# A two-layer attention and expert kernel: the next layer norm's statistics beside the attention's tail, loads reordered, bias products on two row groups, a division shared by two engines

## The chip, the cores and the metric

The kernel runs on one core of a Trainium2 chip. The metric is the device time of one execution in microseconds (us). Beside the times there is one execution recorded by the hardware profiler, from which all durations here come. PE is TensorE's matrix unit and PEld its weight loads, DVE is VectorE, ACT ScalarE, POOL GpSimd, SP SyncE; SP issues most of the transfers.

## The reference

The input x has 2 sequences of 2048 tokens with 256 channels. Two layers follow one another, each of the form

```
xn = layernorm(x)
x  = x + attention(xn) * silu(ffn(xn))
```

```python
# layer 0: full attention over 2048 tokens, 16 heads of 16 channels, scale 1/sqrt(256)
# its ffn: 2 branches of 8 experts of rank 64
xV = einsum('btd,kdr->btkr', Q_side, V);  yW = einsum('btd,kdr->btkr', K_side, W)
prod = xV * cumsum(yW, axis=1)
weights = softmax(gelu(Q_side @ router_w1.T + b1) @ router_w2.T + b2 + expert_bias)
out = einsum('btkr,kdr->btd', prod * weights[..., None], U) + weights @ b
ffn = ((out_fwd + alpha * out_inv) / n_valid) @ W_O.T
# layer 1: attention over the keys at most 64 positions away, scale 1/sqrt(16)
# its ffn: a base product and 8 low-rank experts of rank 16
gate = softmax(xt @ gate_w.T)
ffn  = xt @ weight.T + (1/16) * einsum('ne,eor,ner->no', gate, lora_V, einsum('nh,erh->ner', xt, lora_U))
```

All of it is in 32-bit floats.

## The kernel before

Channels lie on the 128 partitions (two halves, `c`), tokens on the free axis, in blocks of 512 (`TB`): four blocks for each of the two sequences (`b`). Three arrays stay in the on-chip memory: `x`, `xn` (the normed input, later the attention's result) and `gt` (the gate silu(ffn)). A 32-bit product is two passes on TensorE, so the profile counts twice as many matmuls as the code. Tiles come from rotating pools, and an instruction waits until the slot that its tile takes has been read. Each engine works its instructions in a fixed order, and so does each queue of transfers; a scheduler settles this order when the program is built, from the order of the calls, except where `keep_in_program_order` (`pin`) holds an instruction in place.

**Start.** ScalarE's queue loads `wq`, `wiT`, `wk`, `r1T`; SP's queue loads the blocks of x (`load_x`, L54) with the other weights between them. The first products (L204) fold the weights into one another: `wiT` with `wq`, then with `wk`. Beside them `layer_norms` goes over the eight blocks: transposes of x into PSUM (L104), statistics on VectorE (L108 to L115), scaling on ScalarE (L121), transposes back (L127) and copies into `xn` (L129). One of these products multiplies the experts' biases with W_O and gives `bO`, 16 rows. SP then loads the attention's weights and biases and fills rows of the array `qd` in device memory.

**Layer 0's experts.** After the router, a loop over the eight blocks multiplies eight chunks (`px` L387, `py` L391, `po` L371), with the routing weights broadcast from device memory (`we`). Each block ends with two products of `bO` (16 rows) with `wT` (L403), one for each half of the channels, both added into `po`.

**Attention.** `attention` is called once per layer. Its work is cut into 32 items `(b, g, n)`: sequence, group of four heads, block of queries. The four heads sit on partitions 0, 32, 64 and 96. An item has `U` steps, 16 in layer 0, 2 in layer 1. Two streams run side by side: for an item ahead, scores `sq` with queries on the partitions, of which VectorE takes the maxima (L617 in layer 0, the masked `seen` at L612 in layer 1); for the present item, scores `sk` with keys on the partitions (L605), exponentials on ScalarE (L621), in layer 1 masks on POOL (L626), and the products with the values, `acc` (L664). `place_max` transposes an item's maxima (`pmx`, L642), VectorE writes them negated into `row` (L644), and a transfer puts them into the queries as an extra row. In layer 0 the `acc` of the steps are added up in `av`: ScalarE copies each out of PSUM (`more`, L674) and POOL adds it (L675). A table `after`, filled by `at(step, f, ...)`, says behind which step the later parts are called: `away`, `compact`, `invert`, `write`, `spread` and `divide` send an item's sums through device memory and divide (`divide`, L717, on POOL in layer 0, on VectorE in layer 1); `project` multiplies with `wo` (L750), VectorE multiplies with `gt` (L755), POOL adds to x (L756), and in layer 1 the block goes out. The last items (one in layer 0, three in layer 1) are divided by `last_there` and `last_back` instead, with transposes on TensorE (L725, L742).

```python
hops = (0, 1, 3, 4, 5, 7, 8) if local else (0, 2, 4, 5, 7, 11, 13)
...
for s in range(-(U + LEAD), max(after) + 1):
    ...
    scores(divmod(s, U) if 0 <= s < total else None, divmod(s1, U) if s1 < total else None, es)
    ...
    for f, args in after.get(s, []):
        f(*args)
```

With `LEAD` 3, the stream of maxima is `U + 3` steps ahead, so layer 0's last 19 steps have scores `sk`, exponentials and `acc` alone.

**Between the layers.** When the first attention is over, layer 1's weights are loaded, `layer_norms` goes over all eight blocks again, with the gate's logits beside it (`gates` L849, `tokens` L860, `normalized`, `turned` L876), and `turned` sends the gates through device memory to be broadcast (`ge`). Then `experts` takes the blocks: `pt` (L887), the base product (L893), `tg` on VectorE (L889), the second low-rank product (L897), silu on ScalarE (L899). The second attention starts with its keys and queries (`pp`, L456) and values (L469).

Of the kernel before, what the change touches and what calls it, by code (L numbers as in the profile page):

```python
# [17 lines left out]
P = 128  # L18
# [19 lines left out]
def two_layers(ctx: ExitStack, tc: tile.TileContext, a, out):  # L38
# [20 lines left out]
    load_x(0, 0)  # L59
# [13 lines left out]
    def load_attn(pool, l, eng):  # L73
        return dict(
            q=load(pool, f"wq{l}", [P, NC, D], rows(a[f"wq{l}"]), eng),
            k=load(pool, f"wk{l}", [P, NC, D], rows(a[f"wk{l}"]), eng),
            v=load(pool, f"wv{l}", [P, NC, D], rows(a[f"wv{l}"]), eng),
            o=load(pool, f"wo{l}", [P, NC, D], rows(a[f"wo{l}"]), eng),
            bq=load(pool, f"bq{l}", [P, NC], a[f"bq{l}"], eng),
            bk=load(pool, f"bk{l}", [P, NC], a[f"bk{l}"], eng),  # L80
            bo=load(pool, f"bo{l}", [P, NC], a[f"bo{l}"], eng),
            bv=load(pool, f"bv{l}", [P, NC], a[f"bv{l}"], eng),
        )
# [10 lines left out]

    def layer_norms(blocks, tmp, ps, between=lambda r: None):


        QT = TB // P

        def there(b, n):  # L100
            xt = ps.tile([P, QT, D], F32, name="xt", tag="xt")
            for t in range(QT):
                for c in range(NC):
                    nc.tensor.transpose(xt[:, t, bass.ts(c, P)], x[b][:, c, bass.ds(n * TB + t * P, P)], ident)  # L104
            st = tmp.tile([P, QT, 6], F32, name="st", tag="st")
            mv = tmp.tile([P, QT, 2], F32, name="mv", tag="mv")
            for t in range(QT):
                nc.vector.bn_stats(st[:, t, :], xt[:, t, :])  # L108
            for t in range(QT):
                nc.vector.bn_aggr(mv[:, t, :], st[:, t, :])  # L110

            f = tmp.tile([P, 2, QT], F32, name="f", tag="f")
            nc.scalar.activation(f[:, 0, :], mv[:, :, 1], AF.Sqrt, bias=eps_t)
            nc.vector.reciprocal(f[:, 0, :], f[:, 0, :])
            nc.vector.scalar_tensor_tensor(f[:, 1, :], mv[:, :, 0], -1.0, f[:, 0, :], ALU.mult, ALU.mult)  # L115
            return b, n, xt, f
# [15 lines left out]
        for r in range(len(blocks) + 1):  # L132
            first = there(*blocks[r]) if r < len(blocks) else None
            if held:
                back(*held)
            held = first
            between(r)
# [12 lines left out]
    layer0 = ctx.enter_context(ExitStack())  # L150
    wat0 = layer0.enter_context(tc.tile_pool(name="wat0", bufs=1))

# [6 lines left out]
    with tc.tile_pool(name="fw", bufs=1) as fw:  # L159
# [4 lines left out]
        bO = fw.tile([2 * KE, D], F32, name="bO")  # L164
# [4 lines left out]
        with tc.tile_pool(name="raw", bufs=1) as raw, tc.tile_pool(name="tn", bufs=2) as tn, tc.tile_pool(  # L169
# [3 lines left out]
            wq = load(raw, "wq", [P, NC, D], rows(a["W_Q"]), nc.scalar)  # L173
            wiT = load(raw, "wiT", [P, NC, D], rows(a["W_invT"]), nc.scalar)
            wk = load(raw, "wk", [P, NC, D], rows(a["W_K"]), nc.scalar)
# [14 lines left out]
            bT = load(raw, "bT", [P, NC, 2 * KE], rows(a["bT"]), nc.sync)  # L190
# [32 lines left out]
            product(lambda m: bO, bT, 2 * KE, woT)  # L223
# [10 lines left out]
        A0 = load_attn(wat0, 0, nc.sync)  # L234
# [13 lines left out]
        nc.vector.reciprocal(rn, rn)  # L248
        ones = fw.tile([P, TB], F32, name="ones")
# [13 lines left out]
        with tc.tile_pool(name="pa", bufs=2, space=PSUM) as pa, tc.tile_pool(  # L263
# [87 lines left out]
            with tc.tile_pool(name="ta", bufs=2) as ta:  # L351
                for b in range(B):
                    prev = None
                    for n in range(NB):
# [9 lines left out]
                        wT = ta.tile([2 * KE, TB], F32, name="wT", tag="wT")  # L364
                        nc.sync.dma_start(out=wT, in_=wd[b][:, cols])
# [36 lines left out]
                        for oc in range(NC):  # L402
                            nc.tensor.matmul(po[oc], bO[:, bass.ts(oc, P)], wT, start=False, stop=True)  # L403
# [12 lines left out]
    def attention(A, scale, local, final):  # L416
# [14 lines left out]
        with ExitStack() as st:  # L431
# [204 lines left out]
            def place_max(i):  # L636
# [6 lines left out]
                row = mp.tile([NG * TT, P], F32, name="row", tag="row")  # L643
                nc.vector.tensor_scalar(row, ps, -1.0, None, ALU.mult)  # L644
# [5 lines left out]
            def weigh(i, u, es):  # L650
# [17 lines left out]
                if local:  # L668
                    nc.scalar.copy(avs[i][:, bass.ts(u, 2 * P)], acc[:, : 2 * P])
                elif u == 0:  # L670
# [42 lines left out]
            def divide(i):  # L713

                b, g, n = items[i]
                pin(
                    (nc.vector if local else nc.gpsimd).tensor_tensor(together(b, g, n), together(b, g, n), divs.pop(i), ALU.mult)  # L717
                )
# [26 lines left out]
            def project(i, oc):  # L745
# [10 lines left out]
                nc.gpsimd.tensor_tensor(x[b][:, oc, cols], x[b][:, oc, cols], up, ALU.add)  # L756
                if final and oc == NC - 1:
# [12 lines left out]
            for i, (b, g, n) in enumerate(items):  # L770
# [5 lines left out]
                if i >= len(items) - (3 if local else 1):  # L776

                    hops, steps = (0, 1, 2), (last_there, last_back)
                for hop, f in zip(hops, steps):
                    at(end + DEL + hop, f, i)  # L780
# [5 lines left out]
                if n == NB - 1:  # L786
                    at(end, fetch, b * NG + g + 2, T // 2 if local else 0)
            fetch(0)
# [34 lines left out]

    attention(A0, 1.0 / float(np.sqrt(D)), False, False)
    layer0.close()


    wat1 = ctx.enter_context(tc.tile_pool(name="wat1", bufs=1))
    A1 = load_attn(wat1, 1, nc.sync)
    with tc.tile_pool(name="gw", bufs=1) as gw, tc.tile_pool(name="tb", bufs=2) as tb, tc.tile_pool(  # L830
        name="gdp", bufs=1, space=bass.MemoryType.DRAM
    ) as gdp:
        gateT = gw.tile([P, NC, HP], F32, name="gateT")
        nc.vector.memset(gateT, 0.0)
        nc.scalar.dma_start(out=gateT[:, :, :KE], in_=rows(a["gateT"]))
        baseT = load(gw, "baseT", [P, NC, D], rows(a["weightT"]), nc.scalar)
        lU = load(gw, "lU", [P, NC, KE * R1], rows(a["lUT"]), nc.scalar)
        lV = load(gw, "lV", [KE * R1, D], a["lVT"], nc.scalar)
        lg = gw.tile([P, B * NT, KE], F32, name="lg1")
# [3 lines left out]

        def gates(pool, b, n):

            pl = pool.tile([P, P], F32, name="pl1", tag="s")
            for c in range(NC):
                for t in range(TB // P):
                    nc.tensor.matmul(  # L849
                        pl[t * HP : (t + 1) * HP, :], gateT[:, c, :], xn[b][:, c, bass.ds(n * TB + t * P, P)],  # L850
                        start=(c == 0), stop=(c == NC - 1),
                    )
            sl = tb.tile([P, P], F32, name="sl", tag="sl")
            nc.vector.tensor_copy(sl, pl)
            return b, n, sl

        def tokens(pool, b, n, sl):

            pt = pool.tile([P, P], F32, name="plt", tag="s")
            nc.tensor.transpose(pt, sl, ident)  # L860
            t0 = (b * NB + n) * (TB // P)
            nc.vector.tensor_copy(
                lg[:, t0 : t0 + TB // P, :], pt.rearrange("p (t w) -> p t w", w=HP)[:, :, :KE]
            )

        def normalized(b):
            lgb = lg[:, b * NT : (b + 1) * NT, :]
            rec = softmax8(gw, lgb, NT, "g")
            nc.vector.tensor_scalar(rec, rec, 1.0 / R1, None, ALU.mult)
            nc.vector.tensor_tensor(lgb, lgb, rec[:, :, None].to_broadcast([P, NT, KE]), ALU.mult)  # L870

        def turned(pool, b):
            for n in range(NB):
                pw = pool.tile([KE, TB], F32, name="pw1", tag="s")
                for t in range(TB // P):
                    nc.tensor.transpose(pw[:, bass.ts(t, P)], lg[:, (b * NB + n) * (TB // P) + t, :], ident)  # L876
# [6 lines left out]
        def experts(pool, b, n):  # L883
            cols = bass.ts(n, TB)
            pt = pool.tile([P, TB], F32, name="pt", tag="a")
            for c in range(NC):
                nc.tensor.matmul(pt, lU[:, c, :], xn[b][:, c, cols], start=(c == 0), stop=(c == NC - 1))  # L887
            tg = tb.tile([P, TB], F32, name="tg", tag="tg")
            nc.vector.tensor_tensor(tg, ge[b][:, cols], pt, ALU.mult)  # L889
            po = [pool.tile([P, TB], F32, name=f"po1{oc}", tag="o", bufs=4) for oc in range(NC)]  # L890
# [5 lines left out]
            for oc in range(NC):  # L896
                nc.tensor.matmul(po[oc], lV[:, bass.ts(oc, P)], tg, start=False, stop=True)  # L897
                gs = gt[b][:, oc, cols]
                nc.scalar.activation(gs, po[oc], AF.Silu)  # L899

                nc.vector.scalar_tensor_tensor(
                    x[b][:, oc, cols], gs, A1["bo"][:, oc : oc + 1], x[b][:, oc, cols], ALU.mult, ALU.add
                )

        with tc.tile_pool(name="pn1", bufs=2, space=PSUM) as pn1, tc.tile_pool(
            name="pg1", bufs=2, space=PSUM
        ) as pg1:
            blocks = [(b, n) for b in range(B) for n in range(NB)]
            held = {}

            def between(r):
                if r - 1 in held:
                    tokens(pg1, *held.pop(r - 1))
                if 1 <= r <= len(blocks):
                    held[r] = gates(pg1, *blocks[r - 1])
                if r == NB + 1:
                    normalized(0)
                if r == NB + 3:
                    turned(pg1, 0)

            layer_norms(blocks, tb, pn1, between)
# [82 lines left out]
```

## Time and profile before

| | |
|---|---|
| time, median of 3 runs | 2598.02 us (2597.92 to 2598.47) |
| profiled execution: its own time | 2595.75 us |
| its span, first to last instruction | 2594.0 us |
| granted TensorE clock, mean | 0.997 |
| busy: PE, DVE, ACT, POOL | 2543.6, 1681.6, 1633.7, 893.3 us |
| start to the first matmul | 8.21 us |
| layer 0's experts, from 131 on | to 478 us |
| first attention's steps | about 590 to 2121 us |
| layer norm, gates and experts of layer 1 | 2121 to 2236 us |
| second attention's steps | about 2330 to 2573 us |

A row of a view by stages gives a stretch, its length, and the busy time of PE, PEld, DVE, ACT and POOL with the number of instructions, then the granted clock, the share of the DMA engines and GB/s. A row of the timeline gives the start, the duration, the engine, the line, the operation, and in brackets how long the engine had been idle and what ended this. A row of the waits gives who waited for whom, the sum in us, the number of times and the longest.

### The profile page before, as it was taken

The numbers are of one execution on the slowest core, as the hardware profiler recorded it, in microseconds if no ns is written. First come the engines' busy times: TensorE is split into PE (matmuls) and PEld (weight loads), VectorE is DVE, ScalarE is ACT, GpSimd is POOL, SyncE is SP. The second block draws the span as 40 slices with busy tenths as digits, with TensorE's granted clock in tenths as the row PEclk, the third lists the DMA queues.
The fourth block names the chain that finished last, engine by engine and source line by source line (L and its number), as shares of the span: only waits on it lengthen the run. The fifth ranks groups of instructions, "written<-read, shape, count | busy, mean of one in ns | idle before, by whom it ended". The sixth has DMA issues, their size and how long they took to land.

```text
span 2594.0 us, 48140 instructions
## 1 busy us (share of the span) xinstructions
PE 2543.6 (98%) x18916; PEld 1075.1 (41%) x18916; DVE 1681.6 (65%) x2755; ACT 1633.7 (63%) x3188; POOL 893.3 (34%) x836
## 2 busy tenths in 40 slices
PE   8999999999999999999999999999999988999998
PEld 5444444543333333333333333333333325467765
DVE  4143333258888888888777888888888714138875
ACT  5400000127888888888878888888888874236654
POOL 0000000102444444444444444444444440107776
PEclk9999999999999999999999999999999999999999
DMA  7031111320001001010000001010000012234542
GB/s 246 37 85 49 50 49 33 121 74 3 16 10 49 12 11 47 12 44 16 10 22 36 12 21 37 12 46 14 10 16 12 10 34 35 73 123 129 157 143 85
DMA packets 80098, 129.83 MB, mean 50 GB/s; under 512 B 27456, under 2 KB 32448, under 8 KB 77056
## 3 DMA queue, kind: packets, MB, share of 16 engines
q1 hardware_dynamic: 77824, 125.19, 15.4%
q8 instruction: 148, 2.42, 0.4%
q10 hardware_dynamic: 2048, 1.58, 0.2%
q14 instruction: 78, 0.64, 0.1%
HBM read 80.23 MB, written 45.97 MB: 49 GB/s over the span
## 4 chain that ended last, share of the span: by engine, by line
PE 93%; DVE 3%; DMA 2%; ACT 1%; issue 1%; POOL 0%; POOLq 0%; ACTq 0%; SPq 0%; DVEq 0%
PE sk L605 24%; PE acc L664 21%; PE sq L605 18%; PE pp L456 4%; PE py L391 4%; PE po L371 4%; PE px L387 4%; PE pr L750 2%; PE ph L277 2%; PE pp L469 2%; PE psf L204 1%; DVE seen L612 1%; PE po L893 1%; DMA q<-row 1%; PE xb L127 1%
## 5 line engine op out<-in xcount | busy, mean ns | idle before, releaser
L617 DVE TENSOR_REDUCE part<-sq 128x2 f32<-128x1024 f32 x1024 | 1206.6, 1221 | 302.2 <-PE sq L605 301.8
L621 ACT ACTIVATE e<-sk 128x512 f32<-128x512 f32 x2048 | 1063.0, 615 | 215.9 <-PE sq L605 194.2
L605 PE MATMUL sk<-q,k 32*128 32x512 f32 (+2 forms) x5632 | 1153.9, 533 | 12.3 <-DMA q<-row 5.5
L605 PE MATMUL sq<-k,q 32*128 32x512 f32 (+2 forms) x5120 | 1131.4, 569 | 1.3 <-DVE part L617 1.3
L675 POOL TENSOR_TENSOR av<-av,more 128x512 f32<-128x512 f32 x480 | 607.9, 1266 | 962.5 <-ACT more L674 962.4
L605 PEld LDWEIGHTS sk<-q,k 32*128 32x128 f32 x5632 | 530.3, 184 | 604.3 <-ACT e L621 491.8
L664 PE MATMUL acc<-e,v 128*32 128x512 f32 x4096 | 550.6, 605 | 0.0
L605 PEld LDWEIGHTS sq<-k,q 32*128 32x128 f32 x5120 | 403.5, 183 | 22.2 <-DVE part L617 12.2
L674 ACT COPY more<-acc 128x512 f32<-128x512 f32 x480 | 287.8, 600 | 2.5 <-PE acc L664 1.5
L664 PEld LDWEIGHTS acc<-e,v 128*32 128x32 f32 x4096 | 82.5, 108 | 391.5 <-ACT e L621 386.2
L407 ACT ACTIVATE gt<-po 128x512 f32<-128x512 f32 x16 | 9.5, 596 | 324.6 <-PE po L403 324.6
L612 DVE CUSTOM_DVE_ANT_0 seen<-sq,mask 128x256 f32<-128x256 f32 (+1 forms) x512 | 176.7, 408 | 48.7 <-PE sq L605 42.6
L413 POOL TENSOR_TENSOR x<-x,up 128x512 f32<-128x512 f32 x16 | 20.2, 1265 | 459.2 <-DVE up L410 459.2
L626 POOL TENSOR_SCALAR_AFFINE_SELECT xn<-xn 128x512 f32<-128x512 f32 x172 | 110.0, 671 | 90.7 <-ACT xn L621 89.6
L395 DVE TENSOR_TENSOR xs<-we,px 128x512 f32<-128x512 f32 x64 | 43.9, 685 | 136.5 <-PE px L387 135.4
L621 ACT ACTIVATE xn<-sk 128x512 f32<-128x512 f32 x172 | 90.7, 601 | 55.5 <-PE sk L605 26.9
L387 PE MATMUL px<-xn,FV 128*128 128x512 f32 x256 | 121.2, 595 | 0.0
L391 PE MATMUL py<-cum,FW 128*128 128x512 f32 x256 | 120.5, 593 | 0.6 <-DVE cum L360 0.6
L371 PE MATMUL po<-pr,UO 128*128 128x512 f32 x256 | 119.0, 592 | 0.0
L397 DVE TENSOR_TENSOR pr<-xs,py 128x512 f32<-128x512 f32 x64 | 44.0, 687 | 61.3 <-PE py L391 61.1
L755 DVE TENSOR_TENSOR upd<-gt,pr 128x512 f32<-128x512 f32 x32 | 22.0, 687 | 81.4 <-PE pr L750 76.3
L371 PEld LDWEIGHTS po<-pr,UO 128*128 128x128 f32 x256 | 48.6, 190 | 61.2 <-issue 60.5
(167 smaller groups left out, 1634.6 us busy)
## 6 DMA issues: line engine op xcount, KB each, us to landing
we<-wd SPq DMA_DIRECT2D x128, 128.0 KB
ad<-av SPq DMA_DIRECT2D x60, 256.0 KB
qd<-sb SPq DMA_DIRECT2D x48, 256.0 KB
k<-qd SPq DMA_DIRECT2D x10, 1024.0 KB
q<-qd SPq DMA_DIRECT2D x10, 1024.0 KB
xn<-ad SPq DMA_DIRECT2D x60, 128.0 KB
recb<-rd SPq DMA_DIRECT2D x60, 128.0 KB
q<-qd SPq DMA_DIRECT2D x12, 512.0 KB
```

What stands on the lines that cost most here:

```text
L371: nc.tensor.matmul(po[oc], UO[:, ch, bass.ts(oc, P)], pr, start=(ch == 0), stop=False)
L387: nc.tensor.matmul(px, FV[:, c, bass.ts(ch, P)], xn[b][:, c, cols], start=(c == 0), stop=(c == NC - 1))
L391: nc.tensor.matmul(py, FW[:, c, bass.ts(ch, P)], cum[:, c, :], start=(c == 0), stop=(c == NC - 1))
L456: nc.tensor.matmul(ps, w[:, c, bass.ts(hf, P)], xn[b][:, c, bass.ts(n, TB)], start=(c == 0), stop=(c == NC - 1))
L605: nc.tensor.matmul(o, lhs, rhs, start=True, stop=True)
L612: nc.vector.tensor_tensor_reduce(seen[:, lo:hi], sq[:, d, t * 2 * P + lo : t * 2 * P + hi], mask[:, lo:hi], 1.0, LOWEST, ALU.add, ALU.max, ...
L617: nc.vector.tensor_reduce(pt[:, pair[0] : pair[1] + 1, t, kb], sq, AX.X, ALU.max)
L621: nc.scalar.activation(e, t, AF.Exp, scale=scale)
L626: nc.gpsimd.affine_select(out=e[:, :, c, :], in_=e[:, :, c, :], compare_op=ALU.is_ge, fill=0.0, base=0, pattern=[[0, 4], [sign, P]], chann ...
L664: nc.tensor.matmul(acc[hp[j], o : o + hi - lo], vs[b][:, kt, vcols(g, j)], es[j][:, lo:hi], start=(r == 0), stop=(r == len(parts) - 1), sk ...
L674: nc.scalar.copy(more, acc)
L675: nc.gpsimd.tensor_tensor(avs[i], avs[i], more, ALU.add)
```

## The change

- `wq` is loaded by SP as its first transfer, and x's first block follows it. `bT` is held twice, at rows 0 and 32, so that `bO` has two copies of its rows; `wT` is loaded twice as well, and the two products of a block use one copy each.
- One pool `wat` holds the weights of both layers in the same slots. The biases, gate and base weights of layer 1 are loaded at the start; its `wq`, `wk` and low-rank weights at the first attention's step 0, `wo` behind that attention, `wv` behind the experts.
- In the first attention's last 18 steps VectorE adds `acc` to `av` out of PSUM. In every second of these steps half a block of sequence 0 is transposed, copied to `xn` and its statistics taken (`norm_there`). At the end the last item's division and projection are interleaved by hand with sequence 0's scaling, transposes back and gates.
- The stage between the layers treats sequence 1 alone in the same way (`norm_there`, `factors`, `norm_apply`, `norm_back`), with products of `experts` between; `experts` returns its second half as a function to be called later.
- In the second attention the `row` is made by ScalarE, the division of even items by POOL and of odd ones by VectorE. The last four items take `last_there` and `last_back`. The last block is added by VectorE and goes out in two transfers.

```diff
-    load_x(0, 0)
+    def resting(b, n, half):
+        return xn[b][:, half, bass.ts(n, TB)].rearrange("p (t d) -> p t d", d=D)
+    def norm_there(b, n, half, bank, tmp, mv, issue=lambda i: i):
+        H2 = QT // 2
+        xt = bank().rearrange("p (t d) -> p t d", d=D)
+        for t in range(H2):
+            for c in range(NC):
+                i = nc.tensor.transpose(
+                    xt[:, t, bass.ts(c, P)], x[b][:, c, bass.ds(n * TB + (half * H2 + t) * P, P)], ident
+                )
...
+        rest = resting(b, n, half)
+        nc.vector.tensor_copy(rest, xt)
...
+        for t in range(H2):
+            nc.vector.bn_stats(st[:, t, :], rest[:, t, :])
+        for t in range(H2):
+            nc.vector.bn_aggr(mv[:, half * H2 + t, :], st[:, t, :])
+    def norm_apply(b, n, f):
+        for t in range(QT):
+            rest = resting(b, n, t // 2)[:, t % 2, :]
+            if t % 2:
+                nc.scalar.activation(rest, rest, AF.Identity, scale=f[:, 0, t : t + 1], bias=f[:, 1, t : t + 1])
+            else:
+                nc.vector.tensor_scalar(rest, rest, f[:, 0, t : t + 1], f[:, 1, t : t + 1], ALU.mult, ALU.add)
+    def norm_back(b, n, bank):
+        xb = [bank() for _ in range(NC)]
...
-            wq = load(raw, "wq", [P, NC, D], rows(a["W_Q"]), nc.scalar)
+            wq = load(raw, "wq", [P, NC, D], rows(a["W_Q"]), nc.sync)
             wiT = load(raw, "wiT", [P, NC, D], rows(a["W_invT"]), nc.scalar)
+            load_x(0, 0)
...
-                        for oc in range(NC):
-                            nc.tensor.matmul(po[oc], bO[:, bass.ts(oc, P)], wT, start=False, stop=True)
+                        for oc, r in enumerate(twice):
+                            nc.tensor.matmul(po[oc], bO[r, bass.ts(oc, P)], wT[r, :], start=False, stop=True)
...
-                nc.vector.tensor_scalar(row, ps, -1.0, None, ALU.mult)
+                if local:
+                    nc.scalar.activation(row, ps, AF.Copy, scale=-1.0)
+                else:
+                    nc.vector.tensor_scalar(row, ps, -1.0, None, ALU.mult)
...
+                elif i * U + u >= len(items) * U - U - LEAD and u:
+                    nc.vector.tensor_tensor(avs[i], avs[i], acc, ALU.add)
...
-                    (nc.vector if local else nc.gpsimd).tensor_tensor(together(b, g, n), together(b, g, n), divs.pop(i), ALU.mult)
+                    (nc.vector if local and i % 2 else nc.gpsimd).tensor_tensor(together(b, g, n), together(b, g, n), divs.pop(i), ALU.mult)
...
-                nc.gpsimd.tensor_tensor(x[b][:, oc, cols], x[b][:, oc, cols], up, ALU.add)
-                if final and oc == NC - 1:
+                ends = final and i == len(items) - 1
+                (nc.vector if ends else nc.gpsimd).tensor_tensor(x[b][:, oc, cols], x[b][:, oc, cols], up, ALU.add)
+                if ends:
+                    nc.sync.dma_start(out=out[bass.ts(oc, P), bass.ds(b * T + n * TB, TB)], in_=x[b][:, oc, cols])
...
-                if i >= len(items) - (3 if local else 1):
+                if i >= len(items) - (NB if local else 1):
...
+                for r in range(2 * NB):
+                    n, half = divmod(r, 2)
+                    at(total - U - LEAD + 1 + 2 * r, norm_there, 0, n, half, single, op, mv[:, tile_of(n), :], pin)
+                at(total - 1, factors, nf, mv, pin)
...
+            there(0)
+            there(1)
+            factors(nf[:, :, two(0)], mv[:, two(0), :])
+            whole_bias(A1, small())
+            turned(pl, 0)
+            first = experts(0, 0)
+            norm_apply(1, 0, nf[:, :, tile_of(0)])
...
+            tokens(small(), sl[3], 1, 3)
+            normalized(gw, 1)
+            rest = experts(0, 3)
+            turned(pl, 1)
+            rest()
+            for n in range(NB):
+                experts(1, n)()
+    A1["v"] = weight(1, "v")
```

## The prediction

> **What bounds the kernel now.** I read the page's busy shares and its chain first, then a table of busy time by stage, then the timeline at the places that the diff touches, and last the waits of the second attention.
>
> ```profile
> PE 2543.6 (98%) x18916; PEld 1075.1 (41%) x18916; DVE 1681.6 (65%) x2755; ACT 1633.7 (63%) x3188; POOL 893.3 (34%) x836
> ...
> PE 93%; DVE 3%; DMA 2%; ACT 1%; issue 1%; POOL 0%; POOLq 0%; ACTq 0%; SPq 0%; DVEq 0%
> ```
>
> TensorE is busy 98% of the span and is 93% of the chain. So an edit pays only where TensorE waits, or where it takes TensorE work away. The stage table (stretch, length, then busy time of PE, PEld, DVE, ACT, POOL) says where that is:
>
> ```profile
> 174.00:478.00 304.00, 303.31 (x705) 131.88 (x704) 105.09 (x137) 9.67 (x17) 17.77 (x15) 1.00 0.14 43
> ...
> 2066.00:2124.00 58.00, 55.43 (x349) 14.29 (x341) 5.83 (x10) 49.82 (x101) 33.65 (x27) 1.00 0.07 19
> 2124.00:2178.00 54.00, 41.13 (x305) 26.42 (x304) 27.07 (x113) 29.78 (x58) 2.53 (x2) 0.84 0.08 22
> 2178.00:2237.00 59.00, 57.76 (x146) 25.68 (x146) 18.67 (x32) 12.93 (x22) 0.96 (x1) 1.00 0.27 37
> ...
> 2330.00:2555.00 225.00, 211.90 (x3769) 160.44 (x3765) 195.23 (x1024) 139.42 (x292) 161.65 (x242) 1.00 0.44 133
> ```
>
> The expert branch (174 to 478) is full of TensorE work: only less work helps. The second layer norm (2124 to 2178) has 13 us of idle TensorE and a clock of 0.84. In the second attention (2330 to 2555) VectorE is at 87% beside TensorE's 94%. The timeline rows (start, duration, engine, line, operation):
>
> ```profile
> 8.21 3.75 PE L204 MATMUL psf<-wq,wiT 128*128 128x256 f32 x8 [8.21 <-DMA wiT<-in_W_invT]
> ...
> 171.08 1.98 PE L403 MATMUL po<-wT,bO 16*128 16x512 f32 x4
> ...
> 2067.53 1.14 PE L605 MATMUL sk<-q,k 32*128 32x512 f32 x8
> ...
> 2123.42 0.66 PE L725 MATMUL tr<-ident,av 128*128 128x128 f32 x4 [2.57 <-POOL av L675]
> ...
> 2236.53 3.70 PE L456 MATMUL pp<-xn,wk 128*128 128x512 f32 x8 [0.69 <-ACT gt L899]
> ...
> 2348.04 0.28 PE L642 MATMUL pmx<-ident,mx 128*16 128x128 f32 x1
> ...
> 2354.57 0.28 PE L642 MATMUL pmx<-ident,mx 128*16 128x128 f32 x1
> ...
> 2440.90 0.28 PE L642 MATMUL pmx<-ident,mx 128*16 128x128 f32 x1
> ...
> 2448.21 0.28 PE L642 MATMUL pmx<-ident,mx 128*16 128x128 f32 x1
> ```
>
> One `pmx` comes per item (two steps) of the second attention: its period is 6.53 us while no division runs yet (2348.04 to 2354.57) and 7.31 us with them. The rows and waits between say why: VectorE ends an item with division and row, and TensorE's scores need the bank that `row` empties.
>
> ```profile
> 2449.10 0.92 DVE L717 TENSOR_TENSOR xn<-xn,recb 64x512 f32<-64x512 f32 x1
> ...
> 2450.12 0.22 DVE L644 TENSOR_SCALAR row<-pmx 16x128 f32<-16x128 f32 x1
> ...
> 2450.39 0.48 PE L605 MATMUL sk<-q,k 32*128 32x256 f32 x1 [0.29 <-DVE row L644]
> ```
> ```profile
> PEld sk L605 <- DVE row L644: 12.7, 18, 0.9
> ...
> PE sk L605 <- DMA q<-row: 5.5, 4, 1.9
> ```
>
> **What the skill says.** The Trainium skill, TensorEngine Tiling (Array Packing), Key Properties: tiles on different rows run in parallel, and a change of the tiling mode drains the array. The trace agrees: eight passes on four row groups took 1.07 us to the next start (2067.53 to 2068.60), four passes of L403 on one group 1.91 us. DMA: Bandwidth & Descriptors, Queues, rings and completion order: a DMA engine goes round-robin between its queues. Between 4 and 7 us SP's queue moved 0.78 MB and ScalarE's 0.39 MB, nearly equal counts of packets (411 and 403). SBUF — State Buffer, Who interferes with whom: a VectorE operation with two SBUF inputs contends with GpSimd's reads. L717 took 0.675 to 1.131 us, which fits it.
>
> **The change part by part.** The sum is made against the profiled execution, 2595.75 us (span 2594.0); the median of the runs is 2.3 us above it.
>
> (a) First weights. `wq` moves from ScalarE's queue to the head of SP's, ahead of x; `wiT` becomes the head of ScalarE's. Both (0.52 MB) are moved before anything else. By the DMA view of the first 12 us, that much had gone by about 3.9 us; with about 1 us to the release, TensorE starts at 5.1 instead of 8.2. x's first block, now second on SP, has its 0.5 MB by about 7 at 250 GB/s, and is needed at 13. Behind it TensorE is busy 22.0 of 22.1 us, so the shift stays. **-3.0** (0 to -3.5). SP also gets six small DMAs (a second for bT, four biases, the gate) and `baseT`, all ahead of the qd fills, whose readers come 400 us later; ScalarE issues one less. Zeroing bT and the gate costs VectorE under 0.5 us while it waits for x; uncovered, that 0.5: 0.
>
> (b) Bias products. The two L403 products of a block move to two row groups. Now 1.91 us; side by side 2 passes of 0.43 and 0.19 of switching, 1.05. 8 x 0.86 = **-6.9** (0 to -7.5; the passes are the same, so no loss). The product that makes bO has 48 rows for 16 and streams the same 256 columns. The second `wT` DMA, 8 x 32 KB, stands on SP ahead of a block's 16 `we` DMAs and is read at the block's end, some 40 us later: 0, and one issue of 0.31 us a block if that cover were gone.
>
> (c) Tail of the first attention. In its last 19 steps no score maxima are computed. 14 of them are held by ScalarE at 2.45 us (four exponentials 2.06, one copy 0.39). The copy goes; VectorE, 10% busy here, adds out of PSUM, about 0.69 us a step. TensorE alone needs 2.07. So 14 x 0.38 = 5.3 is freed, and eight groups of four transposes at 0.11 with 0.1 of switching (8 x 0.53 = 4.2) come in. VectorE's part of these, a copy (0.69), two statistics (0.70) and two aggregates (0.18) every second step, is 1.6 beside 1.4 of additions in 4.6 us: covered. **-1.0** (+3 to -4).
>
> (d) Between the layers. From the last `acc` (2120.84) to the first `pp` (2236.53) it now takes 115.7 us. After it: first batch 0: addition, transposes and back of the last item, 4.6 us (VectorE's additions replace 2.57 us of waiting on POOL); 32 transposes at 0.11, four products of 0.86, four gates of about 0.9, four token transposes, in all about **17**. Then batch 1, where VectorE is the slowest: 12 copies of 0.65 (7.8), 16 statistics (5.5), aggregates (1.5), 8 scalings of 0.3 (2.4), small operations 4.3, and a softmax at the end with an exponential table (1.28, from the row of L144) that TensorE waits for, 3; with handovers, **26.7**. TensorE's own 19 us, with 8.6 of expert products (10 of 64), hide under that. Then the other 54 expert products, 46.3, and 0.5. Last, in the changed order one of the four `pw` groups of batch 1 stands behind 20 expert products, so its broadcast comes late: from the last `pw` of batch 0 (2174.3) to its `tg` (2188.19) took 14 us, and 12 products, 10 us, cover it: **4**. 17 + 26.7 + 46.8 + 4 = 94.5, so **-21.2**. Not shown before: scalings in place on VectorE, 0.2 to 0.45 each (I take 0.3), and PSUM banks shared two at a time. Bounds -8 (ten more in VectorE's part, 3 more for the broadcast) to -28 (TensorE's work alone, 87). Weight loads of layer 1 stand on SP at the first attention's step 0, in slots whose readers are just done, ahead of a `row` that has 13 steps to spare; `wo` follows the last projection and is needed 7 us later; `wv` waits for the last expert product, ahead of the first qd stores, and is needed 27 us later: 0, or some 3 us for one of them if it came late.
>
> (e) Second attention. `row` goes to ScalarE, about 0.3 in a period where it has 4.8 of work; every other division (0.81) goes to POOL at about 1.28 (the same operation on POOL in layer 0). In the four items from 2341.51 to 2367.47 VectorE was busy 23.20, so 5.8 per item without division; 5.6 without row too, and 6.5 with a division. POOL has 4.8 to 5.3 of masks (19.17 in these four, 26.36 in five from 2389.80), and 1.28 every other item. All are at or under TensorE's 6.5, so I take 6.6. 17 items at 7.35: 17 x 0.75 = 12.7; the four with a projection, 11.0 to 10.4: 2.5. Less 1 for divisions late on POOL and rows late by DMA: **-14** (+2 to -19). What waits behind a division on POOL are the masks of two steps later `acc`, with 3.7 us of slack. `out` no longer stands ahead of `row` on SP.
>
> (f) End. Item 28 takes the transposing way: +1.1 on a full TensorE. The last addition on VectorE (0.69 for 1.27) and a halved last DMA: -1.2. **0** (+1 to -2).
>
> Sum -46.1: 2549.7 for a profiled execution, **2552** as a median.
>
> **Rivals.** *The layers' gap keeps half* (17%): VectorE or the late broadcast takes 10 us more: 2562. For it: copies out of PSUM are added. Against: 27 busy of 54 before. *Divisions and masks make POOL the second attention's bound* (13%): its gain is 0 to 5, 2561 to 2566; 161.65 busy in 225 speaks for it, the alternation against. *The bias products stay serial* (5%), against the 1.07 us above: 2559. *Everything TensorE-bound* (10%): 2538. *Slower* (4%): POOL is in order, and a division waits there for `recb` with the masks behind it. 14 such divisions must each hold the chain by 46/14 = 3.3 us to eat the gain; at 5 us it would be 2598 - 46 + 70 = 2622. Against it: VectorE waited for `recb` once, 1.0 us. No difference, 2%, if several fail together.
>
> **Numbers.** The main case has 49%, with its own range 2543 to 2562. Leaving out the slow case and the far ends, 2532 to 2574. Within 0.2% (5 us, about what a measurement can tell) 0.02, faster 0.94, slower 0.04.
>
> **What would show it.** First matmul near 5 us; L403's successor 1.05 us for its four passes; the last-`acc`-to-first-`pp` distance near 95; `pmx` periods of 6.5 to 6.7; no wait on `row`. It is wrong if the gap stays over 108, if the periods stay over 7.1, or if POOL's division is what `acc` waits for.

## The result, and the profile after

The changed kernel takes 2567.85 us (median of four runs, 2565.11 to 2569.33) beside 2597.97 (2595.76 to 2598.47): a ratio of 0.9884, 95% interval 0.9867 to 0.9902. The profiled execution took 2565.11, its span 2563.3. So 30.7 us went out of the span. The forecast sum was 46.1.

First the busy shares and the chain that ended last, of the kernel after:

```profile
PE 2519.8 (98%) x18928; PEld 1065.6 (42%) x18928; DVE 1688.4 (66%) x2752; ACT 1622.5 (63%) x3182; POOL 882.3 (34%) x830
...
PE sk L662 24%; PE acc L724 22%; PE sq L662 19%; PE pp L513 4%; PE pr L813 2%; PE pp L526 2%; DMA q<-row 1%; PE po L1005 1%; PE po L1013 1%; PE pt L1001 0%; PE pmx L699 0%; PE xb L113 0%; DMA ge<-gd 0%; DVE seen L669 0%; DVE part L674 0%
```

TensorE still leads. Two transfers show in the chain, `q<-row`, which had 1% in the chain of before too, and `ge<-gd`. The first is not one of the engines that the prediction weighed. The stage table of the kernel after (columns as before; tail, rest of batch 0 and batch 1, expert products, second attention):

```profile
2059.00:2116.00 57.00, 55.53 (x377) 16.73 (x373) 31.26 (x71) 45.06 (x88) 10.75 (x9) 1.00 0.04 11
2116.00:2164.00 48.00, 38.37 (x302) 24.57 (x303) 32.53 (x102) 20.29 (x36) 12.38 (x8) 0.91 0.19 30
2164.00:2218.00 54.00, 50.48 (x117) 21.70 (x115) 16.31 (x23) 11.99 (x19) 0.41 (x4) 0.96 0.15 21
2311.00:2536.00 225.00, 213.00 (x3992) 164.03 (x3985) 184.72 (x995) 152.56 (x344) 180.81 (x269) 1.00 0.44 136
```

Between the layers TensorE is idle for 9.6 of 48 us and then 3.5 of 54. In the second attention VectorE fell from 195 to 185 busy and POOL rose from 162 to 181, yet TensorE is idle for 12 of 225. The timeline rows that answer to those of before:

```profile
4.90 3.57 PE L251 MATMUL psf<-wq,wiT 128*128 128x256 f32 x8 [4.90 <-DMA wiT<-in_W_invT]
...
168.80 1.13 PE L457 MATMUL po<-wT,bO 16*128 16x512 f32 x4
169.86 0.28 PE L379 MATMUL pw<-ident,lg 128*16 128x128 f32 x1
...
2115.24 0.66 PE L788 MATMUL tr<-ident,av 128*128 128x128 f32 x4 [1.36 <-DVE av L732]
...
2391.10 0.28 PE L699 MATMUL pmx<-ident,mx 128*16 128x128 f32 x1
2397.63 0.28 PE L699 MATMUL pmx<-ident,mx 128*16 128x128 f32 x1
2399.45 0.48 PE L662 MATMUL sk<-q,k 32*128 32x256 f32 x2 [1.54 <-DMA q<-row]
2405.43 0.28 PE L699 MATMUL pmx<-ident,mx 128*16 128x128 f32 x1
2412.07 0.28 PE L699 MATMUL pmx<-ident,mx 128*16 128x128 f32 x1
```

TensorE starts at 4.9. The four bias passes take 1.06 us to the next start. But the `pmx` periods are not 6.5 to 6.7: they are 6.53, 7.80 and 6.64, and in the long one TensorE waits for a transfer.

Shifts of such landmarks give the bill, in us. Each row is the change in distance from the landmark before it.

| stage, up to | forecast | measured |
|---|---|---|
| (a) first router product (58.21 to 54.77) | -3.0 | -3.4 |
| order of `pw` in the first expert block | 0 | +0.8 |
| (b) eight bias products | -6.9 | -6.9 |
| start of first attention (third group of `pp`, 484.64 to 477.40) | 0 | +2.2 |
| (c) last `acc` (2119.78 to 2112.81) | -1.0 | +0.3 |
| (d) first `pp` of the second attention (2236.53 to 2217.72) | -21.2 | -11.8 |
| first `pmx` | 0 | -0.2 |
| (e) 32nd `pmx` (241.1 to 229.1 apart) | -14 | -12.0 |
| (f) end | 0 | +0.4 |

(d) falls short by most, and (e) came out near its number in another way than forecast. In both rows this execution is also a lucky one. In the experiments that leave the stage of (d) as it is, the last `acc` to `pp` took 104.6 to 107.0 us for the 104.4 here; in those that leave the second attention as it is (6, 7, 8 and 11), `pmx` 0 to 31 took 230.6 to 233.0 for the 229.1 here. So (d) brings 9 to 12 us and (e) 8 to 12.

### The profile page after: what moved, and what is told of

It reads as the page before. It is cut to its first block, busy times and chain, and to the rows that moved or that the text cites. A ratio compares the mean times of both kernels' runs of the same rounds, so it can differ in the third digit from the quotient of the medians.

```text
span 2563.3 us, 48080 instructions
## 1 busy us (share of the span) xinstructions
PE 2519.8 (98%) x18928; PEld 1065.6 (42%) x18928; DVE 1688.4 (66%) x2752; ACT 1622.5 (63%) x3182; POOL 882.3 (34%) x830
## 4 chain that ended last, share of the span: by engine, by line
PE 77%; DMA 2%; DVE 1%; ACT 1%; issue 0%; SPq 0%; POOL 0%; ACTq 0%; DVEq 0%; POOLq 0%
PE sk L662 24%; PE acc L724 22%; PE sq L662 19%; PE pp L513 4%; PE pr L813 2%; PE pp L526 2%; DMA q<-row 1%; PE po L1005 1%; PE po L1013 1%; PE pt L1001 0%; PE pmx L699 0%; PE xb L113 0%; DMA ge<-gd 0%; DVE seen L669 0%; DVE part L674 0%
## 5 line engine op out<-in xcount | busy, mean ns | idle before, releaser
L662 PE MATMUL sk<-q,k 32*128 32x512 f32 (+2 forms) x5632 | 1140.3, 532 | 10.6 <-DMA q<-row 9.8
L738 POOL TENSOR_TENSOR av<-av,more 128x512 f32<-128x512 f32 x462 | 586.0, 1268 | 941.8 <-ACT more L737 941.8
L662 PEld LDWEIGHTS sk<-q,k 32*128 32x128 f32 x5632 | 522.9, 184 | 589.3 <-ACT e L678 482.7
L737 ACT COPY more<-acc 128x512 f32<-128x512 f32 x462 | 270.9, 586 | 1.1 <-issue 0.5
L683 POOL TENSOR_SCALAR_AFFINE_SELECT xn<-xn 128x512 f32<-128x512 f32 x172 | 107.0, 657 | 80.8 <-ACT xn L678 79.7
L444 PEld LDWEIGHTS py<-cum,FW 128*128 128x128 f32 x256 | 48.4, 190 | 61.5 <-issue 59.8
```

Source lines behind the costliest of these rows:

```text
L444: nc.tensor.matmul(py, FW[:, c, bass.ts(ch, P)], cum[:, c, :], start=(c == 0), stop=(c == NC - 1))
L662: nc.tensor.matmul(o, lhs, rhs, start=True, stop=True)
L683: nc.gpsimd.affine_select(out=e[:, :, c, :], in_=e[:, :, c, :], compare_op=ALU.is_ge, fill=0.0, base=0, pattern=[[0, 4], [sign, P]], chann ...
L737: nc.scalar.copy(more, acc)
L738: nc.gpsimd.tensor_tensor(avs[i], avs[i], more, ALU.add)
```

## Experiments

A "distance" is one between TensorE starts in a profiled execution; a ratio is to the kernel before, from timed runs (0.9884 for the changed kernel).

**1. `row`'s transfer on ScalarE's queue.**

```diff
-nc.sync.dma_start(out=q[HD:P:HP, ...], in_=row)
+(nc.scalar if local else nc.sync).dma_start(out=q[HD:P:HP, ...], in_=row)
```

> The changed kernel, with one edit: the transfer of `row` in the second attention is issued by ScalarE, right behind the instruction that makes `row`, and not by SP. Theory A (a transfer is the new bound): on SP the transfer stands behind `recb`'s, which waits up to 3.5 us for the reciprocals to land, behind two readings of `ad`, and every fourth item behind two fetches of 0.5 MB; the scores of the next item wait for it. Then the periods of `pmx` go from 6.5 and 7.8 in turn to about 6.6 throughout, the wait of `sk` for `q<-row` (8.3 us in the ten items before the projections) goes to under 1, and pmx 0 to pmx 31 goes from 229.1 to 218-222 us. Theory B (POOL's masks with divisions, or VectorE, bound the item and the wait is a symptom): periods and the 229.1 stay within 2 us. Theory C (ScalarE has no room for an issue of about 0.6 us per item): exponentials come later, 229.1 grows by 3 or more.

Ratio 0.9850 (0.9834 to 0.9867), median 2559.1. `pmx` 0 to 31 takes 221.1, most periods are 6.3 to 6.8, and the wait for `q<-row` is gone. Theory A. What makes the transfer late in the changed kernel is in SP's rows (start, duration of the issue). The wait that ended at 2399.45 was for a `row` that ScalarE had made by 2391.82 and SP issued at 2394.16; the last row below is the next item's, which ScalarE had made by 2398.35:

```profile
2391.87 0.60 SPq L761 DMA_DIRECT2D xn<-ad  x1
2392.57 0.53 SPq L584 DMA_DIRECT2D q<-qd  x1
2393.14 0.93 SPq L584 DMA_DIRECT2D k<-qd  x1
2394.16 0.59 SPq L705 DMA_DIRECT2D q<-row  x1
...
2395.44 0.59 SPq L751 DMA_DIRECT2D ad<-av  x1
2399.56 0.55 SPq L774 DMA_DIRECT2D recb<-rd  x1
2400.21 0.54 SPq L760 DMA_DIRECT2D dn<-ad  x1
2400.81 1.37 SPq L761 DMA_DIRECT2D xn<-ad  x1
2402.27 0.58 SPq L705 DMA_DIRECT2D q<-row  x1
```

SP works its rows in order. It stood still from 2396.03 to 2399.56 at `recb`, whose source was still on its way to HBM, and issued the second `row` 3.9 us after it was ready. Yet TensorE did not wait for that one: by the semaphore's times in the trace it had landed 2.0 us after its issue. The first was issued 2.3 us after it was ready, right behind the two fetches of the next queries and keys, and landed only 5.2 us after its issue. So it is in all seven waits: the `row` stood 1.2 to 3.3 us on SP, behind two fetches, and then took 4.3 to 5.2 us to land, where those without fetches ahead mostly took 1.7 to 2.2. Such fetches come with every second item, hence the long periods in turn with short ones.

**2. `row` first in its step, still on SP.**

```diff
-at(i * U - LEAD, place_max, i)
+after.setdefault(i * U - LEAD, []).insert(0, (place_max, (i,)))
```

> The changed kernel, with one edit: within a step the `row` transfer is placed on SP ahead of `recb`'s and of the readings of `ad`, still on the same queue as the fetches. Theory A, with the order on SP as the cause: nearly all of the gain of the run with ScalarE's queue, pmx 0 to pmx 31 at 219-223 us. Theory A with the bytes of the fetches as the cause: only items without a fetch get shorter, 224-227. Theory B (an engine bounds the item): 229 within 2.

The edit moves the transpose and the making of `row` to the head of their step too, and in both layers; from the third `pp` group to the last `acc` the first attention takes 1635.4 us with it and without. Ratio 0.9849 (0.9834 to 0.9864), median 2558.9; `pmx` 0 to 31 takes 222.1, so the fetches' bytes alone (224 to 227) are not the cause. A `row` behind two fetches still takes 3.3 to 5.1 us to land, but it is issued as soon as it is made, and no wait for it is left. The order on SP is enough of a cause. The waits of the DMA queue (total us, times, longest), ten items of the changed kernel, then of this one:

```profile
SPq L774 <- DMA rd<-dn: 20.8, 10, 3.5
...
SPq L705 <- ACT av L729: 1.7, 4, 0.6
```
```profile
SPq L705 <- ACT row L702: 17.0, 11, 2.7
...
SPq L774 <- DMA rd<-dn: 0.8, 2, 0.6
```

SP now waits for `row` itself, and while it does `rd` lands, so `recb` waits for next to nothing. The same waiting, put ahead of the other transfer, costs no one anything.

**3 and 4. One half of the edit undone.** In 3 all divisions are on VectorE; in 4 `row` is.

```diff
-(nc.vector if local and i % 2 else nc.gpsimd).tensor_tensor(...)
+(nc.vector if local else nc.gpsimd).tensor_tensor(...)
```
```diff
-if local:
-    nc.scalar.activation(row, ps, AF.Copy, scale=-1.0)
-else:
-    nc.vector.tensor_scalar(row, ps, -1.0, None, ALU.mult)
+nc.vector.tensor_scalar(row, ps, -1.0, None, ALU.mult)
```

> The changed kernel, with the sharing undone: all divisions of the second attention on VectorE, `row` still on ScalarE. If a transfer's place on SP is the bound (theory A), 0.9 us more of VectorE in every other item matters little: 229.1 grows by 0 to 3. If VectorE's load is what bounds an item (theory B, as the prediction had it): two items go from 14.3 to about 14.6-14.9, 229.1 grows by 4 to 8. If POOL bounds it with masks and divisions, taking 1.27 from every other item makes it faster by 3 or more.

> The changed kernel, with the other half undone: `row` made by VectorE (0.22 us), behind what VectorE then has queued; divisions still shared. Theory A: `row` comes later in the items where VectorE also divides, its transfer later by 0 to 1 us, 229.1 grows by 2 to 6. Theory B with VectorE: 0.22 x 31 = up to 7 more. If only the sharing matters, no change within 1.

Undone sharing: ratio 0.9882 (0.9859 to 0.9904), no difference from the changed kernel. Its profile alone would have misled: `pmx` 0 to 31 took 226.2 there, 3 less, but that execution, 2559.3, was the fastest of four (the others 2566.9 to 2571.6). Undone `row`: 0.9895 (0.9881 to 0.9910) and 234.5; the intervals overlap, and the distance is in the range of theory A, but only 1.4 over the longest that kernels with an unedited second attention gave. Neither half is missed much.

**9. Both halves undone** (the two diffs together).

> The changed kernel with both halves of the second attention's edit undone: all divisions and `row` on VectorE. With one half undone the medians were 2568.4 (divisions back) and 2570.7 (`row` back) beside 2567.9 with none, so either half alone seems to take VectorE off an item's bound. Theory A (two bounds, VectorE 6.5 + 0.8 and the transfer's place, and either half leaves the transfer as the bound): with both undone VectorE binds again, periods of 7.3 to 7.4 as before the change, pmx 0 to 31 at 238-242, median 2577-2580. Theory B (the gain in this stage came from elsewhere, such as `out` leaving SP's way or another order): 229-234 as with one half, median 2568-2572.

Ratio 0.9927 (0.9913 to 0.9940), median 2576.6; 239.6 for the distance and most periods with a division 7.26 to 7.48: theory A, with a median 0.4 under its range. The waits of this kernel's second attention, `row` against transfer:

```profile
PE sk L662 <- DVE row L701: 6.7, 20, 0.5
...
PE sk L662 <- DMA q<-row: 0.5, 1, 0.5
```

In the changed kernel the same list has `PE sk <- DMA q<-row` at 9.8 us in 7 waits. So there are two bounds close to each other, VectorE's load and the transfer's late landing. Either half of the edit removes the first, both together no more, and the second then holds. The ratio's change from 0.9927 to 0.9884, some 11 us, is what the edit brings; a change of order on SP brings 9 more.

**5. Transfer on ScalarE's queue, all divisions on VectorE** (diffs of 1 and 3).

> The changed kernel with `row`'s transfer on ScalarE's queue and all divisions on VectorE: does sharing the division pay once the transfer is out of the way? Both shared and with its own queue, pmx 0 to 31 took 221.1. If VectorE is the next bound (5.6 us per item without, 6.5 with a division, and it must hand over to TensorE): 224 to 229. If VectorE has room (what the unshared kernel at 226.2, with `row` on SP, suggests): 220 to 222.5, and POOL's part of the change is worth nothing here.

Ratio 0.9861 (0.9845 to 0.9878) beside 0.9850 with sharing: not told apart, so VectorE has room for its divisions to within the 3 us that these intervals can tell. The profiled execution was the longest of four (span 2566.2, and 229.5 for the distance), and shows what ScalarE's queue can cost:

```profile
ACT xn L678 <- DMA k<-qd: 3.5, 1, 3.5
ACT xn L678 <- DMA q<-qd: 2.9, 1, 2.9
```

`row` goes into a `q` that a fetch fills. Its issue waited for the fetches, 2.9 and 2.3 us after `row` was made, and on ScalarE the next item's exponentials stood behind it. By this one execution SP with `row` first is the safer place; the ratios of experiments 1 and 2 don't tell the two apart.

**6. The last block's bias products serial again.**

```diff
 for oc, r in enumerate(twice):
+    if b == B - 1 and n == NB - 1:
+        r = twice[0]
     nc.tensor.matmul(po[oc], bO[r, ...], wT[r, :], start=False, stop=True)
```

> The changed kernel, with the bias products of the last expert block alone on one row group, as before; the other seven blocks stay side by side. The last block of the changed kernel ended 0.86 us earlier, but then TensorE waited 1.17 us for `gt` (0.69 before) and its first eight `pp` passes ran at a granted clock of 0.54. Theory A (both products end together, so ScalarE's two sigmoids come one behind the other, and the longer gap costs TensorE's clock): the wait goes back to about 0.7, the passes to 0.43 us each, and from the last products' start to the third group of eight `pp` passes the time falls by 1.3 us or more although the products take 0.86 longer. Theory B (the clock fell by chance or for the memset on POOL): the passes stay at half speed and the stretch grows by about 0.4.

The row of the changed kernel at the start of the first attention, then that of this one:

```profile
468.73 5.40 PE L513 MATMUL pp<-xn,wk 128*128 128x512 f32 x8 [1.17 <-ACT gt L461]
```
```profile
467.73 3.70 PE L515 MATMUL pp<-xn,wk 128*128 128x512 f32 x8 [0.69 <-ACT gt L463]
```

From the products to the third `pp` group it took 9.64 in place of 10.96, as theory A says. But the ten profiled executions with side-by-side products fall into two kinds: 10.96 in five of them, 9.27 in the other five, with the same wait of 1.17. So A's wait is right, that it slows TensorE is true half of the time, and B's word "chance" is right too. The two executions with a serial last block, this one and experiment 10's, both took 9.64. On the average serial is then worth some 0.5 us, which no run here can show.

**7. A short fill of `v`.**

```diff
-nc.gpsimd.memset(t, 1.0)
+if local:
+    nc.gpsimd.memset(t[:, :, : H * HV].rearrange("p c (h w) -> p c h w", w=HV)[:, :, :, HD:], 1.0)
+    nc.gpsimd.memset(t[:, :, H * HV :], 1.0)
+else:
+    nc.gpsimd.memset(t, 1.0)
```

> The changed kernel, with POOL filling only the columns of the second attention's `v` that are read as ones (16 of each 17 are written by `values` anyway): 8.3 us of POOL at 2135.7 to 2143.9 become 1 to 2. In the changed kernel the four scalings in place that ran beside it took 0.79 us each, those at 2117 and 2151, with POOL idle, 0.34. Theory A (they contend for SBUF): all are at 0.33-0.36, VectorE's part of batch 1 is 1.8 us shorter, and last `acc` to first `pp` goes from 104.4-105.9 to about 103-104. Theory B (another cause, such as ScalarE's scalings on the same tile): still near 0.79, no change.

The timeline of the changed kernel, POOL's fill and VectorE's scalings in place, then the same scalings here:

```profile
2135.66 8.27 POOL L498 MEMSET v<- 128x4879 f32 x2 [7.86 <-DVE mv L124]
...
2142.20 3.15 DVE L132 TENSOR_SCALAR xn<-xn,nf 128x256 f32<-128x256 f32 x4
```
```profile
2144.81 1.37 DVE L132 TENSOR_SCALAR xn<-xn,nf 128x256 f32<-128x256 f32 x4
```

(One run, 2569.2.) Theory A, with one correction: the 0.79 was a mean. The first scaling took 1.88 and ended at 2144.08, just behind the fill (2143.93); the other three, beside small fills, took 0.50, and 0.41 with POOL idle. The first transposes of batch 1 to the first `L1013` took 31.5 us; in seven profiled executions of kernels with the long fill and the old `pw` it was 33.2 within 0.02 (33.5 in the two others). The total from last `acc` to `pp`, 104.3, hides that: the stretch behind it grew by 1.5, of which 0.7 is a wait that experiment 8 shows.

**8. `pw` in two banks.**

```diff
-pw = pool.tile([KE, TB], F32, name="pw1", tag="s")
+pw = pool.tile([KE, TB], F32, name="pw1", **(dict(tag="l", bufs=2) if b else dict(tag="s")))
```

> The changed kernel, with the four `pw` groups of batch 1 in the two banks of tag l in place of the one of tag s, which also puts the fourth ahead of the expert products and not 20 us behind them. Theory A (bank and order): no wait of TensorE for `gT` between them (0.67 twice), no wait of `tg` for `ge` (2.83 on TensorE), last `acc` to first `pp` down by 3 to 4 from 104.4-105.9, to 101-102.5. Theory B (the broadcast's transfers bind `tg` whenever the last `pw` is made): the wait stays, down by 1 at most.

Changed kernel, then this one:

```profile
2161.98 1.01 PE L989 MATMUL pw<-ident,lg 128*8 128x128 f32 x4 [0.67 <-ACT gT L991]
2163.66 1.01 PE L989 MATMUL pw<-ident,lg 128*8 128x128 f32 x4 [0.67 <-ACT gT L991]
...
2197.70 1.98 PE L1013 MATMUL po<-tg,lUV 128*128 128x512 f32 x4 [2.83 <-DVE tg L1011]
```
```profile
2160.56 3.58 PE L989 MATMUL pw<-ident,lg 128*8 128x128 f32 x16 [2.42 <-DVE lg L959]
```

All four groups run in one go, and the wait of `L1013` for `tg`, 2.8 to 3.8 us in the others, is gone. Last `acc` to `pp` falls from 104.3-107.7 to 99.1, more than theory A's 3 to 4. The ratio, 0.9876 (0.9861 to 0.9891), does not tell it from the changed kernel's: in this profile `pmx` 0 to 31 took 232.7, 3.6 more than in the changed kernel's, with `row` on SP as there, which is within the spread of that stage above.

**11. The tail's copies back on ScalarE.**

```diff
-elif i * U + u >= len(items) * U - U - LEAD and u:
-    nc.vector.tensor_tensor(avs[i], avs[i], acc, ALU.add)
```

> The changed kernel, with the additions of the first attention's tail as before: ScalarE copies `acc` out, POOL adds; the transposes and statistics of the next norm stay in the tail. In the changed kernel the 19 steps from the last maxima take 53.57 us (before 53.31), in turn 2.07 and 2.77 a step. Theory A (the addition on VectorE frees ScalarE's 0.39 a step, and the eight groups of transposes spend what it frees): ScalarE holds a pair of steps at 4.9 (two of 2.45) beside 4.83 now, so the 19 steps stay within +0.3 to +1.5, and the wait for POOL's last addition comes back behind them: last `acc` to the first transposes of batch 1 at 20 to 21 in place of 18.0-18.1. Theory B (ScalarE isn't the bound in the tail, nor POOL behind it): both distances within 0.3. Theory C (transposes and copies add up, since they are not in step): 19 steps at 57 or more.

The last 19 steps took 0.6 longer, in turn 2.07 and 2.83 to 3.04, and the distance to batch 1's transposes was 20.0 for 18.0, with the old wait back:

```profile
2116.94 0.66 PE L785 MATMUL tr<-ident,av 128*128 128x128 f32 x4 [2.57 <-POOL av L735]
```

Theory A. The addition on VectorE is worth about 2.6 us in all, by one execution.

**10. Edits 2, 6, 7 and 8 together.**

> The changed kernel with the four edits that helped where they were made: `row`'s transfer first in its step on SP (-9 alone), the four `pw` in two banks (-5.3 to -7 between the layers), the short fill of `v` (-1.7), the last block's bias products on one row group (-1.3). They lie in different stages, so theory A: they add up, 2567.9 - 17 = 2551, range 2547 to 2555. Theory B (the short fill and the `pw` act on the same wait, and the row's transfer keeps a wait for the fetches' bytes): 2555 to 2559.

Ratio 0.9830 (0.9817 to 0.9844), median 2552.0 (2550.0 to 2553.9): theory A. The total is in the range that adding up gave. Of the four parts only the order on SP was clear of noise in timed runs of its own; that each of the others adds its share is read from distances. Last `acc` to `pp` is 96.5 and `pmx` 0 to 31 is 221.1. This is the best version, and beats the kernel before by 1.7%.

## Why the prediction was right or wrong

**2552 forecast, 2568 measured**: inside the wide range of 2532 to 2574, outside the main case's own 2543 to 2562. The direction and the places of the gain were right; the sum was 15 us too large, in the terms below.

(a) Right for the first matmul, at 4.90. The router's -3.4 is in part luck. In the twelve profiled executions of the changed kernel and its variants the first matmul started within 4.64 to 4.93, but the router's product at 53.3 to 54.8 in six and at 56.8 to 57.4 in the other six: the second group of eight products took 2.0 us in the former and 3.8 in the latter. The one execution of the kernel before, at 58.2, also had 3.8. The mean shift is 2.6, and "so the shift stays" is not shown.

(b) Right: 1.06 for four passes beside 1.91. Six of the seven distances between blocks went from 43.31 to 42.45 or 42.46; the first also holds the `pw` groups. What it missed is behind the last block. Both products end together, ScalarE's two sigmoids follow one another, TensorE waits 1.17 for 0.69, and in the profiled execution the next eight passes took 5.23 us for 3.54: +2.2, where the five executions without the slow passes have +0.5. In the first block the third `pw` now waits 0.67 for its bank.

(c) The term that was mis-sized is above all the transposes' 0.53 for a group. Six of the eight groups cost 0.70 (steps of 2.77 beside 2.07), the other two 0.44 and 0.58: 5.2 for 4.2. And twelve steps had been at 2.45, not 14; with two other steps 4.9 was freed for 5.3. Together that is about the 1.3 by which the part missed.

(d) Of the four terms, 17 was measured as 17.4. **26.7 for batch 1 was 33.2.** "Scalings in place ... 0.2 to 0.45 each (I take 0.3)" was free of POOL in its reasoning: alone they take 0.41, but POOL's fill fell on four of them, 1.7 us by experiment 7. Experiment 8 took 0.6 more, although it moved a fourth group in; with both (experiment 10) the stretch is 30.2. Of the other 3.5, 1.60 in the profile is VectorE waiting for transposes that stand behind eight expert products; that order wasn't varied, and the rest stays open. **46.8 + 4 for experts and broadcast was 53.3.** The late broadcast was foreseen and its wait, 2.83 on TensorE, is under the 4. What the sum left out is the clock: behind the softmax's gap passes ran at half speed (a granted 0.50 from 2160.3 to 2164.4, and four passes of `L1013` in 3.62 for 1.9). Experiment 8 brings this stretch to 48.5.

(e) The failed step is "All are at or under TensorE's 6.5, so I take 6.6". It weighed engines and gave transfers "less 1". The wait for `q<-row` was 9.8 us in this stage. That -12.0 lies near -14 is luck. The ten periods ahead of the projections (the 10th to the 19th) took 72.7 us in all beside 72.9 before, so 7.27 each, over the 7.1 that the prediction named as a sign of being wrong; with `row` first on SP they took 66.5. The seven periods with divisions behind the projections gave 4.7, so 4.9 of the 12.7 for the 17 items came; the four with a projection gave 4.0 for 2.5, and 3.0 came from periods that the sum did not hold. The profile of before had both signs, `PE sk <- DMA q<-row` at 5.5 and `recb` waiting for `rd` on SP; while VectorE makes every item 7.3 long, most of that waiting is hidden (0.5 us of it shows in experiment 9). The rival with POOL as the bound fell: POOL divides in 1.26 to 1.29, taking the divisions away changes nothing, and no `acc` waited over 0.35 for a mask, so the slower rival's queue behind a division didn't form either. "What would show it" asked for no wait on `row`, and so looked at the wrong one of two names: `row` was ready, `q` not.

The rival "the layers' gap keeps half" gave 2562 and is nearest the mechanism of (d): the gap is 103.9 from the end of the last `acc`, 9.4 over the forecast, and VectorE and the broadcast are in it, as it said.

## What to carry to other kernels

When a bound engine is relieved, look next at the small transfer that closes the item's loop: find it on its issuing queue and ask what it stands behind, and what that waits for. On a queue in order, put the transfer that a critical engine waits for ahead of one whose source is still in flight, so that both waits run at the same time, and look at what it lands behind as well as at when it is issued. Price an edit that ends two operations together with the engine that must serve both, and check a distance from one execution against the others before giving it a cause.

## What was not expected of the hardware

**TensorE's clock after short gaps depends on the moment.** After the same wait of 1.17 us the next sixteen passes took 8.67 us in five executions and 6.97 in five. The 1.7 us between them is what about 3.4 us at half speed costs; the granted clock there was 0.54 in the changed kernel and 1.00 in experiment 1's. The Trainium skill, TensorE: Matmul & The Clock Gate, Part 1, What's actually happening, tells of a free-running window of some 3.4 us in which activity is watched, which fits both the length and the chance. It has the clock fall after a whole idle window; here 1.17 us of waiting was enough in half of the executions, and the measurement decides. Whether the wait alone does it, or also the four passes ahead of it with 16 rows each, no run here shows.

**Work on POOL can stop a scaling on VectorE outright.** One scaling of 0.41 us took 1.88 and ended 0.15 behind the fill. Another, at 2115.10, took 0.90 and ended 0.15 behind an addition on POOL. The Trainium skill, SBUF — State Buffer, Who interferes with whom, calls the shared ports an exclusive lock for a whole instruction, and that agrees; the copies out of PSUM beside the same fill stayed at 0.66 to 0.69.
